# Mixture-of-experts FFN: tokens sorted by expert through a table in DRAM, in place of running every token through every expert

## Chip, core and metric

One core of a Trainium2 chip. The time is the device time in microseconds of one execution of the whole kernel; of several runs of the same kernel the median counts. The profile is taken on one execution; TensorE is PE, VectorE is DVE, ScalarE is ACT, GpSimd is POOL, SyncE is SP (it issues the DMA transfers). PEld is TensorE's weight load.

## The reference

One transformer block on 4 batches of 512 tokens of 256 numbers, all float32. Cut to what matters:

```
h = layernorm(x) * (1 + ca) + sa           # scale and shift per batch, from c
x = x + ga * attention(h)                  # 16 heads of 128, causal
h = layernorm(x) * (1 + cb) + sb
x = x + gb * ffn(h)

ffn(x):
  h = x @ down_w + down_b                  # 256 -> 128
  probs = softmax(x @ router_w + router_b - 1e-7 * cost)
  topv, topi = top_k(probs, 2);  gate = softmax(topv)
  for k in 0, 1:
    for e in 0..7:                         # hidden 128,256,384,512,128,256,384,512
      hm = h * (topi[k] == e)              # a token that e doesn't serve enters as zeros
      acc += gelu(gelu(hm) @ w1[e] + b1[e]) @ w2[e] + b2[e]
    out += acc * gate[k]
  out += 0.1 * (gelu(gelu(h) @ shared_w1 + shared_b1) @ shared_w2 + shared_b2)
  return out @ up_w + up_b + gelu(x) @ core_w + core_b
```

The masked-out tokens of an expert are not absent: each enters as a row of zeros and comes out as gelu(b1) @ w2 + b2, a constant of the expert, its *idle* output. So a token gets from an expert it isn't routed to that constant, times the gates of the two experts it is routed to, and from its own two experts the real output times a gate. An expert serves about a quarter of the tokens; the most that one expert has of one batch's 512, by the inputs that the reference draws, is 237.

## The kernel before, in words

**Numbers.** Products that need full precision are made as three passes of the fast float32r form: each operand is split into a rounded part and a rest, and `mm3` (L149 to L153) multiplies low by high, high by low and high by high into the same PSUM tile. A plain float32 matmul gives the same in one instruction that PE executes as several slower steps.

**Attention.** The loop runs over 64 heads in the order groups of 4 heads x 4 batches (n = 0 to 63), so the last four, n = 60 to 63, are batch 3's. Per head: projections; scores and exp in `weights` (L550: DVE maximum and mask L567, ACT exp L577, DVE reciprocal L581, POOL normalising L582); the transposed weights in `turned` (L585: DVE transposes L597, then DMAs that move blocks of 32 into place and back, `moved` and `aT`); their split in `parted` (L610: ACT L614, POOL through `rest`, L159); the product with the values in `mixed` (L619), and `project_out` (L647), which adds to the residual (DVE L669, POOL L671). LAG = 3 heads lie between a head's scores and its product with the values. After the last head of a batch the second layer norm, its modulation (into h2T, the FFN's input with features in partitions, DVE L418 and transposes L448) and the routing of that batch follow.

**FFN.** `all_ffn` (L1038) goes through the batches in turn; each has 20 chunks of 128 hidden units (1 to 4 per expert, experts in the order 3, 2, 0, 6, 4, 5, 1, 7) and the shared expert as the 21st. A chunk is two products over all 512 tokens: `first` (L880) multiplies the batch's gelu(h), split in two (L848 and L159), with w1 in three passes of 512 columns and takes gelu on ACT (L900, L903); `second` (L925), FFN_LAG = 3 chunks later, multiplies that with w2 into the expert's PSUM tile. In batch 0 and in the 8 chunks of WHOLE the second product is one plain fp32 matmul (L940); in the other 36 chunks `parts` (L906) splits the activations (ACT, DVE `al`) and mm3 follows. When an expert is complete, DVE takes off its idle output and multiplies by the gate of every token (L964, zero where it isn't routed) and POOL adds it to the batch's sum `oacc` (L968). The gates come as a row per expert, spread to all partitions by a DMA (L888) from gates_e in DRAM, which `route` (L678) writes. `route` has the experts in 32 partitions and works in pieces between chunks. `idle_output` (L797) computes the constants with 20 one-column products (L802). `core` (L996) and `outputs` (L1013) follow for the batch before, at chunks 4 to 6: gelu(x) @ core_w, the sum @ up_w, times the gate row, plus the residual (POOL L1027), out to DRAM.

**Order of the work.** The order of PE's instructions is written by hand for the whole kernel. From the FFN on, that of DVE, ACT and POOL is written by hand too (`manual_schedule`, L1312 to L1320); before that a scheduler of the framework decides theirs. Each engine works in order, and all DMAs are issued by SP. FFN weights are split early in the attention (PART_AT, `part_wf`), kept in DRAM and loaded back from head n = 60 on and, by LATE_UNITS, during the FFN.

Of the kernel before, what the change touches and what calls it, by code (L numbers as in the profile page):

```python
# [11 lines left out]
F32 = mybir.dt.float32  # L12
F32R = mybir.dt.float32r
AF = mybir.ActivationFunctionType
# [9 lines left out]
HG = 4  # L24
# [15 lines left out]

WHOLE = (1, 3, 6, 8, 11, 13, 16, 18)
PARTED = tuple(i for i in range(NCH) if i not in WHOLE)

# [3 lines left out]
def runs(blocks):  # L47

    out = []
    for x in blocks:  # L50
# [12 lines left out]
    **{  # L63
        f"second{u}": ([N2 + PLACE[i] for i in PARTED[4 * u : 4 * u + 4]], True)
        for u in range(len(PARTED) // 4)
    },
    "whole": ([N2 + PLACE[i] for i in WHOLE], False),
    "shared": ([2 * NCH, 2 * NCH + 1], True),
    "up": ([2 * NCH + 2, 2 * NCH + 3], False),
    "core": (list(range(2 * NCH + 4, 2 * NCH + 8)), True),  # L70
    "down": ([2 * NCH + 8, 2 * NCH + 9], True),
# [19 lines left out]

LAST_USE = {f"second{u}": PARTED[4 * u + 3] for u in range(len(PARTED) // 4)}
LAG = 3
FFN_LAG = 3
FFN_OUT = 6
GELU_PARTS = (17, 19)
FFN_CORE = (4, 5)
BEFORE3 = 4
EARLY = 2
# [13 lines left out]
PART_AT = (17, 19, 21, 23, 25, 27, 35, 37, 39, 41, 43)  # L113

LATE_UNITS = (
    ("first3", "wu", 0),
    ("second2", "aTh", 2),
    ("first4", "wu", 4),
    ("core", "wu", 4),
    ("shared", "T", 5),  # L120
    ("up", "vf", 6),
)

@with_exitstack
def adaln_attention_moe_kernel(
# [107 lines left out]
    gb1 = const.tile([P, NCH], F32, tag="gb1", name="gb1")  # L233
# [3 lines left out]
    wf_t: dict[str, bass.AP] = {}  # L237
# [11 lines left out]
    def part_wf(u: str):  # L249

        n = len(UNITS[u][0]) * P
        st = staged[u]
        d = parts_d[u] = dram.tile([P, 3, n], F32, tag=f"wfp_{u}", name=f"wfp_{u}")
        if u.startswith("second"):
            nc.sync.dma_start(d[:, 2, :], st)
        hi = work.tile([P, 512], F32R, tag="stage", name=f"hi_wf_{u}")[:, :n]
        nc.scalar.copy(hi, st)
        nc.sync.dma_start(d[:, 0, :], f32(hi))
        rest(nc.gpsimd, st.bitcast(F32R), st, hi)
        nc.sync.dma_start(d[:, 1, :], st)  # L260

    def load_wf(u: str, tag: str = "wu"):
        blocks, in_parts = UNITS[u]
        n = len(blocks) * P
        pool, bufs = (const, 10) if tag == "wu" else (work, 3 if tag == "vf" else 2)
        if not in_parts:
            wf_u[u] = pool.tile([P, n], F32, tag=tag, name=f"wf_{u}", bufs=bufs)
            load_runs(wf_u[u], wf_runs(u))
            return
        t = wf_t[u] = pool.tile([P, 2, 512], F32, tag=tag, name=f"wf_{u}", bufs=bufs)  # L270
        wf_u[u] = t[:, 0, :n].bitcast(F32R), t[:, 1, :n].bitcast(F32R)
        if u.startswith("second"):
            nc.sync.dma_start(t[:, 1, :n], parts_d[u][:, 2, :])
        else:
            load_parts(u)

    def load_parts(u: str):
        n = len(UNITS[u][0]) * P
        nc.sync.dma_start(wf_t[u][:, :, :n], parts_d[u][:, :2, :])
# [28 lines left out]
    router_w = const.tile([P, DC, 2 * E], F32, tag="router", name="router")  # L308
# [13 lines left out]
    with tc.manual_schedule(engines=fixed):  # L322
        nc.vector.memset(mask[:, : NT - 1, :], 0.0)
        nc.vector.memset(router_w, 0.0)
    nc.sync.dma_start(router_w[:, :, :E], router.rearrange("p (c n) -> p c n", n=E))
# [110 lines left out]
    def modulated(b: int, which: int):  # L436
# [28 lines left out]
        if which and b:  # L465
            for c in range(DC):
                turn(c)
                yield
                scaled(c)
                yield  # L470
                parts(c)
            yield
            return
# [200 lines left out]
    routed: dict[int, bass.AP] = {}  # L674

    last_exps: dict[str, mybir.Instruction] = {}

    def route(b: int):  # L678


        n = S // R

        def each(a: bass.AP) -> bass.AP:

            return a.unsqueeze(2).to_broadcast([R, n, E])

        def row(a: bass.AP) -> bass.AP:

            return a.unsqueeze(1).to_broadcast([R, n, E])

        def t2(nm):
            return small.tile([P, n], F32, tag=f"r_{nm}", name=f"r_{nm}_{b}", bufs=1)[:R]

        pl = psum.tile([P, S], F32, tag="pj", name=f"pl_{b}", bufs=3)[:R]
        parts = [(c, a) for c in range(DC) for a in h2T[b]]
        for i, (c, a) in enumerate(parts):
            nc.tensor.matmul(
                pl, lhsT=rw[:, c], rhs=a[:, c, :], start=i == 0, stop=i == len(parts) - 1
            )
        yield  # L700
        lt = work.tile([P, S], F32, tag="stage", name=f"lt_{b}")[:R]
        nc.vector.transpose(lt, pl)
        lt3 = lt.rearrange("p (j e) -> p j e", e=R)
        yield
        lg = small.tile([P, n * E], F32, tag="r_lg", name=f"r_lg_{b}", bufs=1)[:R]
        lg = lg.rearrange("p (j e) -> p j e", e=E)
        nc.vector.tensor_tensor(lg, lt3[:, :, :E], lt3[:, :, E : 2 * E], ALU.add)

        ex, s, hot1, gt = (
            lt[:, i * n * E : (i + 1) * n * E].rearrange("p (j e) -> p j e", e=E) for i in range(4)  # L710
        )
        nc.vector.tensor_tensor(lg, lg, row(rbias[:R]), ALU.add)
        yield
        m, sm, f, g1, g2 = (t2(nm) for nm in ("m", "sm", "f", "g1", "g2"))
        desc = rt[:R, R_DESC - R_ROUTER : R_DESC - R_ROUTER + E]

        def top(hot):
# [3 lines left out]
            nc.vector.tensor_tensor(lg, lg, each(m), ALU.subtract)  # L721
            yield
            nc.vector.scalar_tensor_tensor(s, lg, 0.0, row(desc), op0=ALU.is_ge, op1=ALU.mult)
            nc.vector.tensor_reduce(f, s, AX.X, ALU.max)
            nc.vector.tensor_tensor(hot, s, each(f), ALU.is_equal)

        def exp(to, a, spare):


            if b == 0:  # L730
                last_exps["route"] = nc.scalar.activation(to, a, AF.Exp).ins
                return
            nc.scalar.activation(to, a, AF.Tanh, scale=0.5)
            yield
# [4 lines left out]
        yield from top(hot1)  # L739
        yield  # L740
        yield from exp(ex, lg, gt)
        yield
        nc.vector.tensor_reduce(sm, ex, AX.X, ALU.add)
        nc.vector.reciprocal(sm, sm)
        nc.vector.scalar_tensor_tensor(lg, hot1, -BIG, lg, op0=ALU.mult, op1=ALU.add)
        yield
        yield from top(gt)
        yield


        yield from exp(g1, m, g2)
        nc.vector.scalar_tensor_tensor(g1, g1, 1.0, sm, op0=ALU.subtract, op1=ALU.mult)
        yield
        nc.scalar.activation(g1, g1, AF.Tanh, scale=-0.5)
        yield
        nc.vector.tensor_scalar(g2, g1, -0.5, 0.5, ALU.mult, ALU.add)
        nc.vector.tensor_scalar(g1, g1, 0.5, 0.5, ALU.mult, ALU.add)
        nc.vector.tensor_tensor(hot1, hot1, each(g1), ALU.mult)
        nc.vector.tensor_tensor(gt, gt, each(g2), ALU.mult)
        yield  # L760


        ge = s.rearrange("p j e -> p (j e)")
        nc.vector.tensor_tensor(
            ge.rearrange("p (e j) -> p j e", e=E), hot1, gt, ALU.add
        )
        turned_gt = ex.rearrange("p j e -> p (j e)")
        nc.vector.transpose(turned_gt, ge)
        gates_e = dram.tile([E, S], F32, tag=f"gates_e{b}", name=f"gates_e_{b}")
        nc.sync.dma_start(  # L770
            gates_e.rearrange("(k a) (j r) -> (a j) k r", a=R // n, r=R),
            turned_gt.rearrange("p (k r) -> p k r", r=R),
        )
        routed[b] = gates_e


    def w1(i: int):
        return part(wf_u[f"first{i // 4}"], (i % 4) * P, P) if i < NCH else part(
            wf_u["shared"], 0, P
        )  # L780

    def w2(i: int, b: int):

        if i == NCH:
            return part(wf_u["shared"], P, P)
        if i in WHOLE:
            return wf_u["whole"][:, ts(WHOLE.index(i), P)]
        k = PARTED.index(i)
        if b == 0:
            return wf_t[f"second{k // 4}"][:, 1, ts(k % 4, P)]  # L790
        return part(wf_u[f"second{k // 4}"], (k % 4) * P, P)


    idle = const.tile([P, E], F32, tag="idle", name="idle")
    cvec = const.tile([P, 1], F32, tag="cvec", name="cvec")

    def idle_output(e: int, mine: list[int]):  # L797

        pc = psum.tile([P, 1], F32, tag="pj", name=f"pc_{e}", bufs=3)
        for n, i in enumerate(mine):  # L800
            at = PLACE[i]
            nc.tensor.matmul(  # L802
                pc, lhsT=w2(i, 0), rhs=gb1[:, at : at + 1], start=n == 0, stop=n == len(mine) - 1
            )
        nc.vector.tensor_copy(idle[:, e : e + 1], pc)

    def constant():

        b2s = small.tile([P, 2], F32, tag="b2s", name="b2s", bufs=1)
        nc.vector.tensor_reduce(b2s[:, :1], ct[:, C_B2 : C_B2 + E], AX.X, ALU.add)  # L810
        nc.vector.scalar_tensor_tensor(
            b2s[:, :1], ct[:, C_B2 + E : C_B2 + E + 1], 0.1, b2s[:, :1], op0=ALU.mult, op1=ALU.add
        )
        nc.vector.tensor_reduce(b2s[:, 1:], idle, AX.X, ALU.add)
        nc.vector.tensor_tensor(cvec, b2s[:, :1], b2s[:, 1:], ALU.add)
# [11 lines left out]
    begun: dict[int, mybir.Instruction] = {}  # L827

    beside: list = []

    def next_piece():
# [592 lines left out]
```

## Time and profile before

| | |
|---|---|
| runs | 799.51, 801.11, 802.89 us; median 801.11 |
| the profiled execution | 802.16 us, its span 800.4 us |
| mean granted clock of TensorE | 0.991 |
| first score of head n = 63 (PE) | 600.9 us after the span's start |
| first product of the experts (`ph`, PE) | 608.5 us |
| HBM | 73.05 MB read, 50.14 MB written |

Times in the profile's lines count from the start of the span; 1.76 us of the execution lie around it. A line of a group reads: line of the code, engine, operation, output <- inputs with their shapes, how often | busy time, mean duration of one | idle time of the engine just before them, and what ended it. Matmuls are pipelined, so their durations overlap. A line of a table by stretches reads: stretch, its length, then for PE, PEld, DVE, ACT and POOL the busy time and in brackets the instructions, then the granted clock, the share in which the DMA engines were busy, and GB/s. In a DMA line the last number is the median time in us from issue to landing.

### The profile page before, as it was taken

To read this page: it belongs to the slowest core of one execution; us is meant where nothing else is said; L and a number is where in the kernel's file an instruction comes from. 1 tells how busy PE (TensorE), PEld (TensorE's weight loads), DVE (VectorE), ACT (ScalarE), POOL (GpSimd) and SP (SyncE) were. 2 spreads that over 40 slices of the span, in tenths; PEclk is the share of its full clock that TensorE was granted. 3 is DMA by queue.
4 is the path that set the end of the run, shared out by engine and by line. 5 is a ranking of instruction groups with operands and counts; after the bars stand their busy time and mean duration, and the time that the engine had idled before them with its cause. 6 is when DMAs were issued, how large, how long until landed. Compare 5 with 4: busy or idle time off the path is not lost. (4 is left out here: it accounts for less than half of the span.)

```text
span 800.4 us, 14197 instructions
## 1 busy us (share of the span) xinstructions
PE 777.7 (97%) x4530; PEld 675.6 (84%) x4530; DVE 595.1 (74%) x1736; ACT 511.3 (64%) x1211; POOL 504.1 (63%) x495
## 2 busy tenths in 40 slices
PE   8999999999999999999999999998999989989897
PEld 7899999999999989999999999997897756767575
DVE  6897877777776767776777777787985587868855
ACT  5677677767667677667667767666566335656562
POOL 4466657786665778565768767563565355563765
PEclk9999999999999999999999999999999999999999
DMA  7466455756666667666557656444576331302122
GB/s 252 132 179 196 121 160 151 211 162 193 195 183 202 176 208 188 175 185 194 162 172 205 190 155 189 139 138 133 158 229 203 118 98 54 98 35 75 59 70 62
DMA packets 73354, 124.12 MB, mean 155 GB/s; under 512 B 9136, under 2 KB 51392, under 8 KB 73280
## 3 DMA queue, kind: packets, MB, share of 16 engines
q1 hardware_dynamic: 72864, 123.20, 52.2%
q8 instruction: 36, 0.59, 0.3%
q14 instruction: 38, 0.31, 0.1%
q10 hardware_dynamic: 416, 0.02, 0.0%
HBM read 73.05 MB, written 50.14 MB: 154 GB/s over the span
## 5 line engine op out<-in xcount | busy, mean ns | idle before, releaser
L582 POOL TENSOR_SCALAR e<-e,inv 128x128 f32<-128x128 f32 (+3 forms) x256 | 135.7, 539 | 190.8 <-DVE inv L581 183.5
L577 ACT ACTIVATE e<-e,nmax 128x128 f32<-128x128 f32 (+3 forms) x256 | 143.9, 564 | 67.0 <-DVE nmax L567 66.1
L159 POOL TENSOR_TENSOR aT<-aT,aTh 128x1152 fp32r<-128x1152 f32 x64 | 171.2, 2675 | 16.7 <-ACT aTh L614 9.2
L567 DVE CUSTOM_DVE_ANT_0 e<-ps,mask 128x128 f32<-128x128 f32 (+3 forms) x256 | 122.9, 486 | 56.8 <-PE ps L153 40.5
L597 DVE STREAM_TRANSPOSE T<-e 128x384 f32<-128x384 f32 (+2 forms) x256 | 100.8, 446 | 35.2 <-POOL e L582 35.1
L632 ACT CAST zh<-pz 128x512 fp32r<-128x512 f32 x64 | 37.6, 588 | 78.6 <-PE pz L628 78.4
L614 ACT CAST aTh<-aT 128x1152 fp32r<-128x1152 f32 x64 | 73.1, 1141 | 3.9 <-DMA aT<-moved 3.9
L151 PE MATMUL ps<-kh,ql 128*128 128x256 f32 (+2 forms) x192 | 70.9, 369 | 3.0 <-DVE nmax L567 3.0
L151 PE MATMUL po<-wo,zl 128*128 128x256 f32 x256 | 72.8, 284 | 0.4 <-DVE zl L159 0.4
L152 PE MATMUL pv<-wv,hTh 128*128 128x256 f32 x256 | 72.3, 283 | 0.0
L151 PE MATMUL pv<-wv,hTl 128*128 128x256 f32 x256 | 72.3, 283 | 0.0
L153 PE MATMUL po<-wo,zh 128*128 128x256 f32 x256 | 72.3, 282 | 0.0
L153 PE MATMUL pv<-wv,hTh 128*128 128x256 f32 x256 | 71.9, 281 | 0.0
L152 PE MATMUL po<-wo,zh 128*128 128x256 f32 x256 | 71.7, 280 | 0.0
L153 PE MATMUL pz<-aTh,vh 128*128 128x512 f32 (+2 forms) x192 | 65.3, 340 | 0.0
L152 PE MATMUL ps<-kl,qh 128*128 128x256 f32 (+2 forms) x192 | 65.0, 339 | 0.1
L152 PE MATMUL pz<-aT,vh 128*128 128x512 f32 (+2 forms) x192 | 65.0, 339 | 0.0
L151 PE MATMUL pz<-aTh,vl 128*128 128x512 f32 (+2 forms) x192 | 65.0, 339 | 0.0
L153 PE MATMUL ps<-kh,qh 128*128 128x256 f32 (+2 forms) x192 | 64.8, 338 | 0.0
L968 POOL TENSOR_TENSOR oacc<-oacc,part 128x512 f32<-128x512 f32 x28 | 39.8, 1422 | 38.2 <-DVE part L964 33.6
L581 DVE RECIPROCAL inv<-tot 128x1 f32<-128x1 f32 x256 | 39.8, 157 | 30.4 <-ACT e L577 25.0
L159 DVE TENSOR_TENSOR zl<-pz,zh 128x512 fp32r<-128x512 f32 x64 | 43.8, 684 | 16.4 <-ACT zh L632 16.4
(240 smaller groups left out, 2335.1 us busy)
## 6 DMA issues: line engine op xcount, KB each, us to landing
moved<-T SPq DMA_DIRECT2D x256, 160.0 KB, 2.8
aT<-moved SPq DMA_DIRECT2D x64, 640.0 KB, 3.9
spread<-gates_e SPq DMA_DIRECT2D x32, 256.0 KB, 3.2
st_wqk<-in_wqk SPq DMA_DIRECT2D x16, 256.0 KB, 4.2
wf_first<-wfp_first SPq DMA_DIRECT2D x5, 512.0 KB, 4.5
st_wv<-in_wv SPq DMA_DIRECT2D x8, 256.0 KB, 4.2
st_wo<-in_wo SPq DMA_DIRECT2D x8, 256.0 KB, 3.5
wmod<-in_wmod SPq DMA_DIRECT2D x6, 256.0 KB, 4.4
```

The source lines that it names most:

```text
L151: nc.tensor.matmul(o, lhsT=wl, rhs=mh, start=start, stop=False)
L152: nc.tensor.matmul(o, lhsT=wh, rhs=ml, start=False, stop=False)
L153: nc.tensor.matmul(o, lhsT=wh, rhs=mh, start=False, stop=stop)
L159: return eng.tensor_tensor(lo, full, f32(hi), ALU.subtract)
L567: least = nc.vector.tensor_tensor_reduce(out=et, in0=ps[:, :n], in1=maskf[:, S - n :], scale=-SCALE, scalar=BIG, op0=ALU.add, op1=ALU.min, ...
L577: exp = nc.scalar.activation(et, et, AF.Exp, bias=nm[:, t : t + 1], scale=-1.0, accum_out=tot[:, t : t + 1])
L581: nc.vector.reciprocal(inv[:, one], tot[:, one])
L582: by_sum = nc.gpsimd.tensor_scalar(et, et, inv[:, one], 1.0, ALU.mult, ALU.mult)
L597: nc.vector.transpose(to[:, first : first + n], blocks[:, at : at + (n - 1) * step + 1 : step])
L614: nc.scalar.copy(hi, full)
L632: recent["z"] = nc.scalar.copy(zh.rearrange(by_block, a=NB, r=R), pz).ins
L968: recent["added"] = nc.gpsimd.tensor_tensor(oacc, oacc, to, ALU.add).ins
```

## The change

Each batch's tokens are placed by expert in a table of 8 x 256 rows of 128 numbers in DRAM, and an expert works only on its 256 rows. The steps, per batch:

- `clear` (twelve DMAs in all, from head n = 36 on, one per head) fills the tables with zeros. Place 0 of each expert stays empty: it yields the idle output.
- `down_and_route`: h = x @ down_w + b stays unsplit (dF), and `route` now has tokens in partitions: 16 products of 16 columns, one step after the other without pieces. It gives gates, and for each token the two experts (hot2).
- `by_token` transposes h so that a token is a row (dtok); `bring` computes each token's place by products with a triangle and with ones (the count of tokens before it with the same expert), and sends the rows to the table with eight indirect DMAs, issued by POOL, 128 rows of 512 bytes each. It also notes whether an expert has more than 255 tokens.
- `Sparse`: per pair of experts `get` reads 512 rows back with four DMAs (runs of 128 bytes), `turn` transposes them on DVE, takes gelu (ACT), and splits (DVE). A chunk is three passes of 256 columns; the second product is two plain fp32 matmuls of 128 x 128 with the activations as weights, so its output has tokens in partitions. A pair's output goes by one DVE copy and one DMA to a second table, `given`.
- `take`: eight indirect DMAs, issued by POOL, fetch each token's two rows; ACT and DVE scale and add them. `add_idle` adds, in one PSUM tile, the idle outputs times (1 - gate) (one plain fp32 product) and the transposed rows, to the shared expert's output.
- The dense path over all 512 tokens stays as `all_experts`, in a branch at the very end that runs only if an expert had more than 255 tokens of a batch; a flag is reduced, loaded into a register on each engine and compared.

Around it: the second weights aren't split any more (unsplit loads, seven splits in PART_AT for eleven), `idle_output`, the spread gates, L964 and L968 are gone; `manual_schedule` for DVE, ACT and POOL in the FFN is gone, so that a scheduler orders them there too; PE's order is still written. The norm, routing and `bring` of batches 0 and 1 lie among the last heads of the attention, those of 2 and 3 among the chunks of batches 0 and 1. `take(0)` comes at chunk 26 of 80, `take(1)` at 46, `take(2)` at 66, `take(3)` behind the last.

```diff
+PLACES = 256
+    def bring(b: int):
...
+        nc.tensor.matmul(pp, lhsT=tri, rhs=mn, start=True, stop=False)
+        for t in range(NT - 1):
...
+        places[b] = small.tile([P, 2 * NT], I32, tag="places", name=f"places_{b}", bufs=B)
+        nc.vector.tensor_copy(places[b], at_sum.rearrange("p k t -> p (k t)"))
+        for t in range(NT):
+            for k in range(2):
+                sent = nc.gpsimd.indirect_dma_start(
+                    table[b][:, :],
+                    bass.IndirectOffsetOnAxis(ap=places[b][:, k * NT + t : k * NT + t + 1], axis=0),
+                    dtok[b][:, t, :],
+                    None,
+                ).ins
...
+    class Sparse:
+        def get(self, i: int):
+            for a in range(NB):
+                nc.sync.dma_start(
+                    got[a * R : (a + 1) * R].rearrange("r (j l) -> r j l", l=R),
+                    table[self.b][i * S : (i + 1) * S, a * R : (a + 1) * R].rearrange(
+                        "(j r) l -> r j l", r=R
+                    ),
+                )
+        def turn(self, i: int):
+            nc.vector.transpose(full, self.got[i])
+            nc.scalar.activation(full, full, AF.Gelu)
+            nc.vector.tensor_copy(hi, full)
+            rest(nc.vector, lo, full, hi)
+        def second(self, k: int, hid, acc):
+            for t in range(tiles):
+                nc.tensor.matmul(
+                    acc[:, half * self.n + t * L :][:, :L],
+                    lhsT=hid[:, ts(t, P)],
+                    rhs=w2(k),
...
+            nc.vector.tensor_copy(y, acc)
+            nc.sync.dma_start(given[self.b][i * S : (i + 1) * S, :]...
+    def take(b: int):
+        for t in range(NT):
+            for k in range(2):
+                nc.gpsimd.indirect_dma_start(
+                    y[:, k, t, :],
+                    None,
+                    given[b][:, :],
+                    bass.IndirectOffsetOnAxis(ap=places[b][:, k * NT + t : k * NT + t + 1], axis=0),
+                )
+            nc.scalar.activation(y[:, 0, t, :], y[:, 0, t, :], AF.Copy, scale=g[:, 0, t : t + 1])
+            nc.vector.scalar_tensor_tensor(y[:, 0, t, :], y[:, 1, t, :], g[:, 1, t : t + 1], ...
+    def add_idle(b: int, also: str = ""):
+        nc.tensor.matmul(po, lhsT=idle[0], rhs=lefts[b], start=True, stop=got is None)
+        for t in range(NT if got is not None else 0):
+            nc.tensor.matmul(
+                po[:, ts(t, P)], lhsT=got[:, 0, t, :], rhs=ident, start=False, stop=t == NT - 1
+            )
+        nc.vector.tensor_tensor(sums[b], sums[b], po, ALU.add)
...
         if b < 2:
             later.setdefault(n + 3, []).append((modulate, b, 1))
-        if b == 0:
-            later.setdefault(n + 4, []).append((all_of, route, b))
+            later.setdefault(n + 4, []).append((down_and_route, b))
+            later.setdefault(n + 5, []).append((by_token, b))
+            later.setdefault(n + 6, []).append((bring, b))
...
-    ctx.enter_context(tc.manual_schedule(engines={DVE, Activation, Pool}))
...
+    nc.vector.tensor_reduce(flags[:, :1], over, AX.X, ALU.max)
+    nc.vector.tensor_copy(flag, flags[:, :1])
+    missing = nc.values_load(flag[:1, :1], min_val=0, max_val=1)
+    with tc.If(missing > 0):
+        all_experts()
```

## Prediction

> **What bounds the kernel now.** I read the page's busy table first, then the granted clock, the busy time by stretches of the FFN, the forms of the FFN's matmuls, the chain that ended last with the timeline behind it, and the waits.
>
> ```profile
> span 800.4 us, 14197 instructions
> PE 777.7 (97%) x4530; PEld 675.6 (84%) x4530; DVE 595.1 (74%) x1736; ACT 511.3 (64%) x1211; POOL 504.1 (63%) x495
> ```
>
> PE is busy 97% of the span; nothing else is over three quarters. The stretches of the FFN (length, then busy time of PE, PEld, DVE, ACT, POOL, then clock and DMA):
>
> ```profile
> 600.00:610.00 10.00, 8.95 (x53) 7.57 (x52) 7.28 (x24) 6.80 (x14) 7.87 (x8) 1.00 0.81 278
> 610.00:630.00 20.00, 19.63 (x113) 15.64 (x110) 5.62 (x10) 10.37 (x15) 6.52 (x3) 1.00 0.38 107
> ...
> 667.00:707.00 40.00, 37.09 (x160) 26.94 (x158) 36.49 (x72) 24.21 (x40) 23.99 (x19) 1.00 0.25 80
> 707.00:747.00 40.00, 38.51 (x160) 28.06 (x160) 29.70 (x49) 21.04 (x36) 20.25 (x16) 0.96 0.16 53
> 747.00:793.00 46.00, 43.09 (x193) 31.98 (x191) 29.78 (x38) 27.61 (x44) 32.61 (x25) 1.00 0.20 64
> 793.00:800.40 7.40, 1.99 (x8) 1.44 (x8) 3.31 (x8) 0.00 (x0) 1.40 (x2) 1.00 0.21 71
> ```
>
> PE leads in each but the last. Only between 667 and 707 does DVE come near it (36.5 of 40). DVE, ACT and POOL have some 5 to 20 us of slack per batch, because PE is slow: that cover is what the change takes away.
>
> ```profile
> L151 PE MATMUL ph<-ghh,wf_first 128*128 128x512 f32 x80 | 42.1, 526 | 1.6 <-DVE ghh L848 0.8 <-ACT hid L900 0.8
> L940 PE MATMUL acc<-hid,wf_whole 128*128 128x512 f32 x64 | 33.6, 607 | 0.5 <-DVE part L964 0.5
> ```
>
> Durations in these rows overlap; what counts is the step from one issue to the next. The timeline gives .233 us for a pass of 512 columns (603.21, 603.44, 603.67), .118 for 256 (790.39, 790.51, 790.63), .86 for a plain fp32 matmul of 512 columns (two records) and .21 for one of 128.
>
> **PE's sum.** The stage starts with the first score of the last head (n=63), at 600.9, and ends at 800.4: 199.5 us. A chunk costs PE 3 x .233 = .70 for its first product and .86 (44 chunks) or .70 (36) for its second; after the change 3 x .118 + 2 x .21 = .78 for both. Eighty chunks: 119.1 before, 62.4 after. Twenty columns for idle tokens (L802, about 3 us) go. New in the stage are add_idle (4 x 1.7), turn_gates (4 x .44), by_token (3 x .44), router products of 16 columns instead of 512 (about level) and prefix matmuls (3 x .6). down, shared, core, up and the last heads stay; down and routing of batch 0 move ahead of head 63 and make 3.4 us there. Adding each matmul in its written order at these steps gives 172.8 us before and 123.0 after. The stage had 199.5 - 172.8 = 26.7 us without an issue: 8.3 behind the last expert, 18.4 spread. Kept as it is, that would make 800.4 + 3.4 - 49.8 = 754. So the question is how much waiting is added.
>
> **What takes PE's place.** In the new stage, from the first sparse chunk on, I add each queue by nearest rows. DVE: per batch four transposes of 128x512 (.69, L702 has 32x512 in .693), four hi copies, four lo differences and four y copies (.69 each, L848), in all 11 us, with the sums, gates and outputs and two late norms and routings: 96 us. ACT: 20 gelus of 256 columns (half of L900's .684 and its fixed part, .42), 4 of 512, core, shared: 73. POOL: 37 us of additions (L994, L975, L1027: 1.3 to 1.5 each) and 56 indirect transfers. PE: 112. Four queues within a factor of 1.5, each waiting on the others in order, replace one that led by far.
>
> **The price of an indirect transfer, g.** No indirect and no POOL-issued DMA is in the trace. The nearest rows:
>
> ```profile
> L413 POOL TENSOR_TENSOR rstd<-rstd,minus_half 128x4 f32<-128x4 f32 x7 | 7.5, 1065 | 0.4
> L159 POOL TENSOR_TENSOR aT<-aT,aTh 128x1152 fp32r<-128x1152 f32 x64 | 171.2, 2675 | 16.7 <-ACT aTh L614 9.2
> ...
> moved<-T SPq DMA_DIRECT2D x256, 160.0 KB, 2.8
> ...
> gates_e<-lt SPq DMA_DIRECT2D x4, 16.0 KB, 1.4
> ```
>
> Below, an issue on SP takes .32 us; above, POOL's longest instruction takes 2.7. I take g = 1.1, next to a slow small POOL operation (1.065), and 2 us of landing between the 1.4 and 2.8 of the last two rows. With it POOL has 37 + 62 = 99 us. A hold-up by DVE would come on top: with both inputs in SBUF, DVE's al takes 992 ns instead of the 692 of ghl from PSUM, so sharing with POOL already shows.
> [...]
>
> **The sum.** I followed the written order of PE and the in-order queues of the others, each at its row.
> 1. Start of head 63: +8.5 (600.9 to 609.4). 3.4 us is PE's moved work; the rest is 9 us more of DVE (second norm, modulation and routing of batch 1 now in heads 60 to 63; between 580 and 600 DVE was 16.45 of 20 us busy) and eight scatters of bring(0), 8.8 us, in front of the normalisations (L582) in POOL's queue. Those 183.5 us that POOL waited at L582 give room for part. Without room it is +13, with all hidden +3.4.
> 2. Turn to the experts: before, chunks fill the last heads' waits from 608.5. After, the first chunk needs the table read back (1.4 to 2.8 landing), transposed, through gelu and split, behind head 63's 18 us of DVE work. PE has 11 us for it: 7.5 idle, first sparse chunk at 628.
> 3. The middle: 98 us of PE's work to the last expert matmul. The scatters of batch 1 (8.8 and 2 landing) hold DVE, which waits in order at the first transpose of batch 1, so the shared expert of batch 0 comes about 10 late. By batch 2's first chunk 77.5 us pass for 54.5 of work; from there 9 more for the gathers of take and the tables of batches 2 and 3. Together 32 idle, 18.4 before.
> 4. Tail: last expert matmul at 758; copy of y .7, its write 2, eight gathers 8.8, landing 2, scale and combine 1, add_idle, core and up of batch 3 to the output's landing 8.5 = 23, with 14 of PE's work in it: 9 idle, 8.3 before.
>
> ```profile
> 788.78 0.86 PE acc L940 x2
> 790.41 0.76 DVE part L964
> 791.32 1.29 POOL oacc L968
> 793.16 2.01 PE py L1022 x8
> 795.65 0.87 DVE y L1035
> ```
>
> This is the present tail, from the chain of waits; the gathers stand in place of the one POOL addition.
> So 800.4 + 8.5 - 49.8 + (7.5 + 32 + 9 - 26.7) = 780.9. The profiled run took 802.16, 1.76 more than its span, 1.05 over the median of 801.11. With the 1.76 I get 782.7, on the median's scale **782 us**, 2.4% faster. About 28 of the 56 indirect transfers lie on this path (4 of bring(0), 8 each of bring(1), one take in the middle, take(3)), so each .1 us of g is worth 2.8 us: 760 at .32, 827 at 2.7, 801 (no change) at 1.8.
>
> **Free edits, and their covers.** The clearing writes, 4.7 MB more on SP's queue from n=36 on, lie beside DMA at 52% mean; 12 issues of .32 to .43 are hidden unless the moved and aT transfers (landing 2.8, 3.9) come later, at worst +1 a piece, 12. Reading the tables, 64 transfers of 128-byte runs: gates_e with such runs landed in 1.4, but 64 KB has four times its runs, so 1.4 to 2.8 and at worst 4 us more at each of four first tables. Fewer weight splits and .32 issues: below 1 us gained. Flag and branch at the end: one DVE reduction and copy (.15 to .3 each) and a load of a register: .5 to 2, beside the last outputs' landing. The order that a scheduler gives DVE, ACT and POOL instead of the written one: -5 to +15, in the range, 0 in the sum.
> A clock drop is the other cost of idling: behind PE's wait at 703 to 707 passes ran at .43 instead of .233 (710.34, 710.77, 711.20) and the stretch shows .96. Three such waits cost some 1.5 to 2 us each, but where PE waits anyway they are hidden; 0 to +5.
>
> **Rivals.**
> A. The indirect transfers cost about .5 us and the waits stay as before: PE bounds, and 754 + 1.8 = 756, to 765. For it: POOL's total slack. Against: step 2 needs no g to be idle.
> B. Slower. One mechanism: an indirect transfer holds POOL for 2 us or more, each scatter and gather in front of its additions; POOL then has 37 + 112 = 149 us in the stage and leads it. It decides from g = 1.8 on; at 2.0 to 2.7 it gives 807 to 827, 812 likeliest. For it: POOL's rows are the longest in the trace. Against: those rows move 1152 elements per partition, an indirect transfer's list 128 numbers.
> C. The cross waits of DVE's new order decide with g near 1.4: 790 to 799, a gain below 2%.
> D. Not what it says: an expert with over 255 tokens in a batch calls the dense path, at least 80 x 1.56 = 125 us behind all: over 900. The reference's inputs, routed, give at most 237, so 1%.
>
> **Chances.** Forecast (766 to 789) .45, A .20, C .15, B .14, no change (797 to 805, between C and B) .05, D .01. Half a per cent, 4 us, is about what a measurement tells from no change. Faster .45 + .20 + .12 (C below 797) = .77; same .03 + .05 = .08; slower .15. The range of 8 in 10 takes in A's 753 and C, and B to 810.
>
> **What would show it.** Right: first sparse ph 19 us behind head 63's first score; PE near 90% busy but with holes of 5 to 10 us at batch 1's first transposes and at the end; POOL's indirect transfers about 1.1 us apart; last expert matmul near 758. A: PE without holes, gathers .5 apart. B: POOL with no gaps from bring(1) on and everything late behind it. Wrong altogether if head 63 begins later than 615, where the attention, not the FFN, was hurt.

## The result, and the profile after

The changed kernel takes **846.9 us** (four runs, 842.5 to 847.7) where the kernel before took 800.3 beside it: a ratio of **1.057 (1.052 to 1.061)**. Forecast were 782, with a range to 810; it went to the other side. The profiled execution took 846.27 us, its span 844.6.

The head of the page, to be held against the one of before:

```profile
span 844.6 us, 14869 instructions
PE 760.2 (90%) x4771; PEld 689.9 (82%) x4771; DVE 581.0 (69%) x1812; ACT 492.7 (58%) x1221; POOL 502.5 (59%) x522
```

TensorE's busy time fell by 17.5 us only and the span grew by 44. The groups of instructions show that the chunks became as small as was planned (80 chunks, passes of 256 columns, two products of 128 x 128 per chunk, each of which makes two records: the 256 of L991 below and 64 more with `wf_second_up`):

```profile
L991 PE MATMUL acc_s<-wf_second,hid_s 128*128 128x128 f32 x256 | 44.8, 304 | 1.7 <-DVE y_s L1001 1.7
L144 PE MATMUL ph_s<-gxh_s,wf_first 128*128 128x256 f32 x80 | 31.2, 390 | 35.4 <-DVE act_shared L1062 22.0 <-DVE gxh_s L966 5.4 <-DVE zl L152 4.0
...
L832 POOL DMA_INDIRECT table<-dtok,places x32 | 31.4, 980 | 22.2 <-DVE places L828 13.6 <-issue 8.5
L1088 POOL DMA_INDIRECT taken<-given,places x32 | 30.8, 962 | 18.3 <-DMA given<-y_s 9.1 <-issue 8.8 <-PE ph_s L146 0.3
```

The first product of a chunk now stands behind 35 us of waiting; before it was 1.6. An indirect transfer holds GpSimd .96 to .98 us, and .30 more pass before the next: 1.26 from one to the next, in runs of eight (10 us) or sixteen (20 us).

The busy time by stretches, cut at the marks of the prediction (head 63's first score, first sparse chunk, last expert product; columns as shown of before):

```profile
612.70:639.30 26.60, 14.06 (x86) 12.89 (x85) 21.57 (x77) 13.19 (x27) 15.21 (x13) 0.81 0.72 194
639.30:814.20 174.90, 126.58 (x834) 117.38 (x835) 85.89 (x197) 71.93 (x156) 81.25 (x77) 0.82 0.32 75
814.20:844.60 30.40, 19.03 (x93) 15.11 (x90) 10.64 (x20) 2.05 (x5) 11.47 (x12) 0.77 0.21 63
```

In the middle no engine is near full: TensorE 127 of 175 us, and part of that at half clock (granted .82 over the middle; .50 from 635.95 to 649.6, where passes of 256 columns stand .21 us apart, against .12 behind that). Here is the account by stage that all that follows uses, read at the same marks in each trace, in us:

| kernel | head 63 starts | turn | middle | tail | span |
|---|---|---|---|---|---|
| before | 600.9 | 7.7 | 183.9 | 7.9 | 800.4 |
| forecast | 609.4 | 18.6 | 130 | 23 | 781 |
| after | 612.7 | 26.5 | 175.0 | 30.3 | 844.6 |
| after_third (same kernel, another chip) | 611.4 | 25.3 | 152.3 | 31.5 | 820.5 |

The turn is the time from the first mark to the second, the middle from the second to the third, the tail what follows. In after the middle gave 9 us where 54 were forecast, and the start, the turn and the tail cost 12, 19 and 22. TensorE's waits from the turn on, from the view of waits of after (in total, times, longest):

```profile
PE ph_s L144 <- DVE act_shared L1062: 22.0, 4, 13.4
PE ph_shared L144 <- ACT hid_s L922: 11.0, 2, 10.8
PE po L144 <- DVE r_g L705: 7.2, 1, 7.2
PE ph_s L144 <- DVE gxh_s L966: 5.4, 1, 5.4
```

Two of these waits are over 10 us long (13.4 and 10.8). The tail, from the chain that ended last:

```profile
814.88 0.34 DVE taken L1096
...
827.02 0.35 DVE taken L1096
827.37 2.05 issue
829.49 1.09 DVE taken L1096
...
835.43 1.71 PE py L1170 x8
837.25 0.76 DVE y L1183 x2
838.00 0.58 DVE y L1185
```

Where before there were two operations and an output, a batch is combined, turned and projected twice (batches 2 and 3), the second time behind its gathers.

### The profile page after: what moved, and what is told of

Its sections match the earlier page's. It is cut to its first block, busy times and chain, and to the rows that moved or that the text cites. A ratio compares the mean times of both kernels' runs of the same rounds, so it can differ in the third digit from the quotient of the medians.

```text
span 844.6 us, 14869 instructions
## 1 busy us (share of the span) xinstructions
PE 760.2 (90%) x4771; PEld 689.9 (82%) x4771; DVE 581.0 (69%) x1812; ACT 492.7 (58%) x1221; POOL 502.5 (59%) x522
## 4 chain that ended last, share of the span: by engine, by line
PE 76%; DVE 8%; DMA 4%; issue 3%; ACT 3%; another core or an unknown queue 3%; POOL 1%; SPq 1%; DVEq 0%; ACTq 0%; POOLq 0%
PE ps L144 4%; PE ps L145 4%; PE ps L146 4%; PE pz L144 3%; PE pz L145 3%; PE pz L146 3%; PE acc_s L991 3%; PE pk L145 3%; PE pk L146 3%; PE pk L144 3%; PE pv L144 3%; PE pv L145 3%; PE pv L146 3%; PE po L144 3%; PE po L146 3%; PE po L145 3%
## 5 line engine op out<-in xcount | busy, mean ns | idle before, releaser
L152 POOL TENSOR_TENSOR aT<-aT,aTh 128x1152 fp32r<-128x1152 f32 x64 | 171.4, 2678 | 14.7 <-ACT aTh L586 7.3
L922 ACT ACTIVATE hid_s<-ph_s,cols 128x256 f32<-128x256 f32 x80 | 37.1, 474 | 59.0 <-PE ph_s L146 32.5
L144 PE MATMUL ph_s<-gxh_s,wf_first 128*128 128x256 f32 x80 | 31.2, 390 | 35.4 <-DVE act_shared L1062 22.0
L553 DVE RECIPROCAL inv<-tot 128x1 f32<-128x1 f32 x256 | 40.1, 159 | 30.2 <-ACT e L549 24.9
```

Of the source, the lines that this page charges most:

```text
L144: nc.tensor.matmul(o, lhsT=wl, rhs=mh, start=start, stop=False)
L152: return eng.tensor_tensor(lo, full, f32(hi), ALU.subtract)
L553: nc.vector.reciprocal(inv[:, one], tot[:, one])
L922: nc.scalar.activation(hid, ph, AF.Gelu, bias=b1[:, PLACE[k] : PLACE[k] + 1])
```

## Experiments

Theory at first: the indirect transfers cost more than their own time; in stretches with them the end of an instruction reaches its waiter late (a *late signal* from here on: an engine stands idle although what it waits for ended microseconds ago). Rivals: it is GpSimd's time that counts; it is the waits that the new structure has anyway; it is the half clock behind the waits. A fifth suspect was the clearing. From the timeline of SyncE's queue in after:

```profile
5.63 2.98 SPq L766 DMA_DIRECT2D table<-mask  x4
14.61 6.54 SPq L766 DMA_DIRECT2D table<-mask  x8
```

The clearing writes are not at head 36 and later, where they are written, but at the very start: nothing on SyncE's queue held them back. The heads lag before by 2.1 us at head 4 and 6.3 at head 8, and keep it.

**Clearing held back.** In e3 the clearing waits behind a late aT transfer:

```
-        nc.sync.dma_start(aT, ...)
+        recent["aT"] = nc.sync.dma_start(aT, ...).ins
...
+        with tc.issue_after(recent["aT"]):
             nc.sync.dma_start(rows_t..., mask...)
```

> The changed kernel with the twelve zero-filling transfers queued on SyncE behind those of heads 36 on, where the code has them, and not at the kernel's start, where the trace has them (5.6 to 21 us). If their place delays the first loads and with them the first eight heads, the lag of head 8 (6.3 us) goes to about 1 and the whole to 841 us (5 to 6 less than 846.9). Rival: the lag of the first heads has another cause, or the fill costs as much among the later heads: within 2 us of 846.9.

Measured: 820.1, ratio 1.023 (1.019 to 1.028), 27 us less than after. That was too much for 6 us of lag, and no late signal was left in the trace.

**Plain transfers.** In e1 SyncE moves the same bytes in fixed rows (the placing by expert is left out), in e2 GpSimd, in e7 SyncE with e3's clearing:

```
-    nc.gpsimd.indirect_dma_start(table[b][:, :], bass.IndirectOffsetOnAxis(ap=places...), dtok[b][:, t, :], None)
+    nc.sync.dma_start(rows_j[2 * t + k], dtok[b][:, t, :])    # e2: nc.gpsimd; the gathers likewise
```

> The changed kernel with its 64 indirect transfers replaced by plain ones of the same size and row length (128 rows of 512 bytes, spread over the whole table), issued by SyncE. It leaves out the placing by expert: tokens go to fixed rows. Theory 1 (while GpSimd issues indirect transfers, the end signals of TensorE's matmuls reach the other engines late, by up to 9 us, and the clock halves in the waits): 780 to 800 us, no wait of ScalarE on a matmul that ended 5 us before. Theory 2 (the order of the queues and the waits between them cost it, whoever issues the transfers): 825 us or more, holes in TensorE like those of the changed kernel. In between if both hold.

> The 64 transfers plain as in the run issued by SyncE (810 us; no placing by expert), but issued by GpSimd. If an indirect transfer costs as GpSimd's own transfer: within 8 us of the changed kernel of this call. If it's the list of rows that costs: within 8 us of 810.

> Plain transfers on SyncE and the late fill together (no placing by expert). If both count by themselves: 810 - 6 = 804 us, 16 below the late fill with indirect transfers; that difference is then what GpSimd's issuing costs. Rival: the late fill's gain of 27 us was mostly the end of late signals, which plain transfers have not either: 804 all the same, so only the heads' lag tells; if it is above 809, the fill costs among the later heads.

Measured: e1 809.8, ratio 1.010 (1.007 to 1.013); e2 815.2, 1.016 (1.012 to 1.020); e7 804.3, 1.003 (1.001 to 1.005). No late signals in any. Issued by GpSimd instead of SyncE the same plain transfers cost 5 us, by runs on two chips; e2's trace also has an operation of VectorE held for 10.5 us (more on such holds below), e1's middle none of over 2.5. Against e3, e7 is 16 us less: the price of indirect transfers on GpSimd, the index and the issuing engine together. And e7, free of all that, is no faster than before: the work that TensorE was spared is eaten by something else.

**Bursts in the kernel before.** e4 adds eight indirect gathers (unused) in GpSimd's queue in batches 1 to 3, e5 as much plain GpSimd work in the same place:

```
+                if b and k == 9:
+                    burst(b)    # e4: 8 x indirect_dma_start; e5: a memset and 7 multiplications
```

> The kernel before with eight indirect loads of 128 rows of 512 bytes, whose data nobody uses, issued by GpSimd in one go at chunk 9 of batches 1, 2 and 3. Theory 1: signals of TensorE come late in the 10 us of each burst, with holes of 3 to 8 us in TensorE: 812 to 825 us, and at least 6 us above the same kernel with plain GpSimd work in the same place. Theory 2: the burst costs only GpSimd's time, 10 us three times, nearly all hidden: 800 to 806, as with plain work.

> The control of the former: in place of each burst one memset and seven multiplications of 128x512 on GpSimd (about 10 us). Both theories: 800 to 806 us; above 806, the hold of GpSimd's additions itself costs TensorE time, and the burst has to be read against this number.

Measured: 821.4, ratio 1.023 (1.020 to 1.027), and 816.6, 1.019 (1.015 to 1.022). Without late signals, 9 to 10 us of GpSimd's time cost some 5 to 6 us of the path each, in the old kernel, of whatever kind. So the hold on GpSimd alone is a price. The indirect kind adds 5 us in three bursts, each of which is also longer (about 10 us against 9).

**Same kernels, another chip.** After once more, on chip 5, and e6, which is e3 with the shared expert's gelu in SBUF so that the next third chunk gets its PSUM tile sooner:

```
-        nc.scalar.activation(ph, ph, AF.Gelu, bias=b1[:, NCH:])
+        act = work.tile([P, S], F32, tag="tmp", name=f"gelu_shared_{b}")
+        nc.scalar.activation(act, ph, AF.Gelu, bias=b1[:, NCH:])
```

> The changed kernel once more, unaltered, beside the others of this call. In its trace ScalarE's gelus start up to 9 us after the matmul that they wait for, while GpSimd issues indirect transfers; in the variant with the late fill, whose FFN has the same instructions in nearly the same order, none do, and its FFN is 24 us shorter. If the early fill makes that: 847 us again, with such late starts. If it belonged to that execution or that chip: 825 to 830 us (the late fill's 820 and the first heads' 6).

> The changed kernel with the late fill, and the shared expert's gelu written to SBUF and not in place in PSUM, so that the next chunk's matmul has the PSUM tile when ScalarE's gelu ends and needn't wait for VectorE's split. In the late fill's trace TensorE waits 13.6 us in four places for that split. If these waits are a cause: 806 to 812 us. Rival: the late signals and gathers decide and the next wait takes their place: 817 to 823.

Measured: 845.2, ratio 1.053 (1.049 to 1.057), and 838.6, 1.044 (1.040 to 1.048), both with late signals. I read this at first as a property of the program, since e3 and e4 had none; but those two had run on chip 11. The next four went to chip 11 together:

> The changed kernel as it is, a third time, on the same chip and beside e3_again. The late signals (an end on TensorE, VectorE or ScalarE that its waiter sees 2 to 11 us later, in stretches with indirect transfers) were in every trace of the changed kernel and of e6_shared_sbuf, and in none of e3_clear_late and e4_before_burst; but the first two ran on other chips than the last two. If the lateness belongs to the program: 843 to 848 here with late signals, and e3_again without them. If it belongs to the chip that a program falls on: both with or both without; without them 822 to 828 here (that is 820 and the 6 us of the early clearing).

> The kernel of e3_clear_late (clearing behind the heads, the rest as the change has it) once more, on the chip of after_third. Lateness by program: 816 to 823, no late signal. Lateness by chip: as late as after_third, 836 to 842 with late signals if after_third has 845, and 816 to 823 without them if after_third has 825.

Measured: after_third **823.5**, ratio 1.028 (1.025 to 1.031); e3_again 817.3, 1.020 (1.018 to 1.021). Neither has a late signal. The unchanged kernel is 22 us faster on this chip; the kernel before is level on all (800 to 802). So it is the chip, or the occasion, together with indirect transfers: late on chips 5 and 2 and in the first run (its chip is not on record), in every kernel with indirect transfers; not late on chip 11; and never with plain transfers (chips 11, 5 and 9). The clearing at the start costs 6 us, the difference of the two.

What a late signal looks like, first in after (all engines' timeline, the tokens' transposes of batch 2). A row gives start and duration; in brackets stands the engine's idle time before it and what ended that, "remote" where the profile shows no sender:

```profile
703.57 0.92 PE L802 MATMUL ptk<-ident,dF 128*128 128x128 f32 x4
...
704.61 0.96 POOL L1088 DMA_INDIRECT taken<-given,places  x1 [0.30 <-issue]
...
712.25 0.47 ACT L922 ACTIVATE hid_s<-ph_s,cols 128x256 f32<-128x256 f32 x1 [7.15 <-remote]
...
715.80 0.69 DVE L804 COPY dtok<-ptk 128x512 f32<-128x512 f32 x1 [10.22 <-remote]
```

then the same instructions, in the same order, in after_third:

```profile
698.15 0.66 PE L802 MATMUL ptk<-ident,dF 128*128 128x128 f32 x4
...
698.84 0.69 DVE L804 COPY dtok<-ptk 128x512 f32<-128x512 f32 x1 [1.73 <-PE ptk L802]
```

The copy follows the transposes within .03 us there; in after it starts 11.3 us behind their end, and VectorE is idle for the last 10.2 of these, while GpSimd's gathers run on at 1.26 us each. From the records I can say that the semaphore is seen late (7 to 12 us at worst, by trace); what delays it they do not show. The traces with late signals also lack records: e2's trace has 1,024 landing signals for its 64 plain transfers, 16 for each; for the 64 indirect ones after's trace holds 248 (248 to 276 in every trace with late signals), after_third's 1,021. Every timed run was recorded, so whether the recording itself has a part in the delay was not tested.

**The half clock.** In e3_again 51 us of TensorE's work run at half clock from 578 us on. e8 fills eight of the waits with unused products:

```
+        for _ in range(n):
+            nc.tensor.matmul(pw, lhsT=ident, rhs=ident, start=True, stop=True)    # n = 28, 20, 20, 20, 9, 9, 20 and 6 + 16
```

> e3_clear_late, with plain 128x128 multiplications of the identity (their results unused) in front of eight of TensorE's waits: 28 before the first product of head 62's second part behind the last head (a wait of 6.3 us), 20 before the first sparse chunk (4.7), 20, 20, 9 and 9 before the four chunks that wait for the shared expert's split (4.7, 4.6, 2.2, 2.2), 20 before batch 1's core product (4.7), 6 and 16 in the tail. At .21 us each they fill the waits and are no longer than these. If the half clock behind the waits costs time: in e3_clear_late 46 us of TensorE work run at half clock; some 28 of them lie behind these eight waits, so 10 to 14 us less, a ratio to e3_again of .983 to .988. If the other engines set the pace there and TensorE only waits elsewhere for what it gains: within 3 us of e3_again, or later by some of the 30 us of added products.

Measured: 824.9, ratio 1.029 (1.027 to 1.031), 8 us **later**. The middle, first in e3_again, then in e8:

```profile
633.60:784.90 151.30, 126.38 (x834) 117.08 (x835) 92.95 (x197) 72.08 (x154) 81.26 (x77) 0.86 0.37 87
```

```profile
640.30:792.00 151.70, 134.66 (x990) 125.15 (x991) 90.39 (x198) 70.19 (x153) 79.52 (x76) 0.94 0.37 86
```

The clock went from .86 to .94, and the middle took the same 151 us; TensorE only waited elsewhere for what it gained: less the 78 products added there (.21 us each, 16 us) its busy time fell from 126 to 118 us. Of the 8 us that the whole lost, 5 are the turn, where the added 28 products were longer than their wait (30.9 us instead of 26). In after the granted clock is .50 behind TensorE's waits of 4.9 to 13.4 us (the 5.38 us before 639.28 among them), but also behind one of 2.09 us (before 826.70), and not behind one of 2.17 (before 749.55). This case shows, as far as e8 filled the waits, that the fall need not cost anything.

**Gathers or scatters; the shared split; the table's way.** e9 is e3 with plain gathers and indirect scatters, e13 is e7 with e6's edit, e14 is e7 without its scatters:

> e3_clear_late, with the 32 gathers of take as plain transfers of 64 KB on SyncE's queue (rows in a fixed order, so the outputs are not combined by token), and the 32 scatters still indirect on GpSimd's. From e3_clear_late (820) to e7_sp_late (804), where both are plain, 16 us went. If the gathers hold the path, three at 8 to 10 us in line behind the scatters or at the end: 806 to 809. If the scatters do, in front of the tables that the first products of each batch need: 814 to 818. On a chip or in a program with late signals both are later by their share of some 20 us, which then goes with the kind of transfer that is left.

> e7_sp_late (clearing late, all transfers plain and on SyncE's queue, no placing by expert, so no late signals on any chip so far) with the shared expert's gelu in SBUF, so that the next third chunk gets its PSUM tile one operation after the product. In e7_sp_late TensorE waited 11.6 us in four places for that split. If these waits are on the path: ratio .990 to .996 (793 to 797). If the other engines set the pace and the wait moves elsewhere: 1.000 to 1.006.

> e7_sp_late with the 32 scatters left out: the tables keep their zeros, so the experts work on zeros, but with the same reads, transposes, gelus, splits, products and gathers. What goes is the chain by which a batch's first tables wait for the routing: scatter, its landing, reading. If that chain sets the turn and the heads of the batches: the turn 19 to 21 us instead of 25, the middle 8 to 15 us shorter than 143, ratio .975 to .985 (782 to 790). If the engines' in-order work (two norms and routings, splits, the batches' ends) sets them, with or without tables: ratio .996 to 1.004.

Measured: e9 814.6, ratio 1.015 (1.014 to 1.017), 3 us less than e3_again, so that of the 13.5 us between e3_again and e7 (1.020 to 1.003) some 10 go with the scatters, or with what else changes with them: in e9 one operation of VectorE is held for 6.8 us, in e7's middle none. e13 800.1, ratio .998 (.996 to 1.000): 4 us less than e7, between the two expectations. e14 799.4, .998 (.995 to 1.001): 4 to 5 us less than e7, with the turn as long as ever (25.8) and the middle 7 shorter; head 63 began 3.9 us later, for a reason not looked into. With the scatters goes, by the edit, the order that kept the work beside the chunks behind them. The account by stage:

| kernel | head 63 starts | turn | middle | tail | span |
|---|---|---|---|---|---|
| e3_again | 607.6 | 26.0 | 151.2 | 30.2 | 815.1 |
| e9_gather_direct | 607.5 | 24.8 | 151.6 | 28.3 | 812.3 |
| e7_sp_late | 605.1 | 25.0 | 143.1 | 26.1 | 799.2 |
| e13_sp_shared | 605.3 | 24.8 | 138.7 | 27.8 | 796.6 |
| e14_no_scatter | 609.0 | 25.8 | 136.2 | 25.8 | 796.8 |

**Three repairs.** They fell on chip 2, with late signals, and so can be compared with each other only. e10 moves batch 1's routing and scatter into the FFN, e11 takes the core's bias off GpSimd, e12 is both with e6's edit:

```
-        if b < 2:
+        if b < 1:    # e10; batch 1: {0: next(m1) twice, 1: down_and_route, 2: by_token, 4: bring} beside the chunks
...
-            nc.gpsimd.tensor_tensor(xu, xu, pair(gbias), ALU.add)
+            nc.tensor.matmul(py[:, t, :], lhsT=ones[:1], rhs=obias[0][:1], start=False, stop=False)    # e11
```

> The kernel of e6_shared_sbuf once more (clearing behind the heads, the shared expert's gelu into SBUF). There it ran among late signals, 838 with the changed kernel at 845. On a chip without them e3_clear_late has 817 to 820 with 10.5 to 13.6 us of TensorE's waits for the shared split in it. If these waits are on the path: 808 to 812. If the other engines' queues set the pace, as e8_warm suggests, and the wait only moves: 815 to 822. With late signals again 836 to 843.

> e3_clear_late with batch 1's modulation, routing, turn and scatter in the first five chunks of the FFN instead of in heads 62 and 63 and behind them. If VectorE's routing of batch 1, ahead of the last head's work in its order, is what makes the turn 25 us instead of the 18.6 of the prediction: the wait of 6 us at the product of head 62's second part goes, the first sparse chunk comes 18 to 20 us behind head 63's first score, and the whole takes 808 to 814, if the scatter of batch 1 stays early enough for its first chunk. If the turn is set by batch 0's own chain (its table's way back, transpose, gelu, split): 24 us and within 3 us of 817 to 820; if batch 1's tables then come late, 820 to 828.

> e3_clear_late with the core's bias added to the accumulator by a plain product of a row of ones with the bias row on TensorE (16 of 256 columns, .43 us each, 7 us), instead of multiplied by the gate and added to x by GpSimd (12 operations, 13 us of GpSimd). In the trace of after_third VectorE's split of batch 1's core input (128x512) took 7.08 us from 759.22, while GpSimd ran six of these additions back to back (758.40 to 765.74); TensorE waited 7.8 us for it. If additions of GpSimd on SBUF keep VectorE's operations on SBUF out, and this sits on the path: that split takes 1.3 or less, the wait goes, 809 to 813. If not: the split stays long, or the time within 3 us of 817 to 820.

> e3_clear_late with the edits of e6_shared_sbuf, e10_one_later and e11_bias_by_pe together. If each of the three waits is on the path, 5 to 8 us each: 797 to 803, level with the kernel before (802). If the middle is set by GpSimd's runs of scatters and gathers (16 in line, 20 us, twice) and by the order of VectorE: 808 to 816.

Measured: 840.9 (ratio 1.049, 1.047 to 1.051), 848.8 (1.058, 1.055 to 1.061), 852.9 (1.063, 1.058 to 1.067) and 858.8 (1.074, 1.070 to 1.079). None helps. In e10 the turn is 22.0 instead of 25.7; the wait for r_g (6.4 us in e6_again) has become one of 6.0 us for another operation of VectorE, zl. But the middle is 13 us longer than in e6_again (which also has e6's edit). Batch 1's first chunk does not wait for its tables; it is the first five chunks, with batch 1's routing now beside them, that take 24.4 us instead of 14.7. In e11 no operation of VectorE is held for the core's bias any more (below), but the tail took 39 us, with 17 us of TensorE's work in it at half clock. What these edits give on a chip without late signals was not tried.

The hold that e11 was made for, in after_third, GpSimd's and then VectorE's timeline:

```profile
758.40 7.34 POOL L1142 TENSOR_TENSOR x<-x,gbias 128x512 f32<-128x512 f32 x6
```

```profile
759.22 7.08 DVE L152 TENSOR_TENSOR gxl<-gx,gxh 128x512 fp32r<-128x512 f32 x1
```

A subtraction that takes .69 us elsewhere takes 7.08, until GpSimd's run of six additions is over. On chip 2 the order differs and another operation is held, in e6_again (VectorE's, then GpSimd's timeline):

```profile
762.17 8.05 DVE L1098 SCALAR_TENSOR_TENSOR taken<-taken,g 128x128 f32<-128x128 f32 x1 [0.23 <-ACT taken L1097]
```

```profile
762.70 7.37 POOL L1144 TENSOR_TENSOR x<-x,gbias 128x512 f32<-128x512 f32 x6
```

In e10 the same one takes 7.50. In e11 and e12, on the same chip and without these additions, no operation of VectorE takes more than 2.7 us from head 63 on. And in e7, beside the run of six from 707.39 to 714.82, VectorE's operations with an input in PSUM go through in their usual time:

```profile
713.30 0.69 DVE L1108 TENSOR_TENSOR sum<-sum,po_idle 128x512 f32<-128x512 f32 x1 [2.30 <-PE po_idle L1105]
```

So VectorE was held for a whole run of six (7.08 and 8.05 us), not for the rest of one addition (1.25 us).

## Why the prediction was wrong

Point by point, by its own steps; after_third is the kernel without late signals.

- **g, the price of an indirect transfer: right.** 1.26 us from one to the next against 1.1; at the 28 transfers put on the path this is 4.5 us. Below the 1.8 at which rival B decides, so the slowdown is not B. VectorE did not hold the transfers up: their issues took .94 to 1.31 us, beside whatever VectorE did (after_third).
- **PE's work: right in kind, short in size.** Middle: 123.4 us busy, 33 of them at half clock, make 107 at full clock (123.4 - 33/2), forecast 98.
- **Step 3, "together 32 idle": this step failed.** The middle took 152.3 us in after_third, 22 over the forecast of 130. 9 are the work above, 13 more are lost time: 45 us instead of 32. Of the 45 TensorE is idle for 29, and 16 are what the half clock adds; they are counted together because e8 made less of the one, got as much more of the other and gained nothing. Taken away step by step, scatters by index were worth 8 us of the middle (e9 to e7), the way through the table 7 (e7 to e14), the shared expert's split in PSUM 4 (e7 to e13). The prediction had the first two and no term for the third, nor for VectorE held by GpSimd's additions (an operation of 7.1 us in after_third). What this last is worth is not shown: in e7 it is gone too, and may be part of the 8, and e11 ran among late signals only.
- **And it had no term for late signals**: on the chips of the result another 22.7 us, all in the middle (175.0 against 152.3; the other stages differ by 1.3 at most). No row of before could show them, since it has no indirect transfer. It is half of what the middle missed, and a third of the whole miss (844.6 against 781).
- **Step 2, the turn: mis-sized, 25 to 26.5 us instead of 18.6.** The prediction let VectorE's 18 us of work for head 63, with the first table's way back behind it, set it. The way back does not: e14 has no scatter to wait for and the same turn. VectorE's queue has a part in it: it is busy 21 of the turn's 25.3 us in after_third, and with batch 1's routing moved out (e10) 12.9 of 22.0. One of its operations, of .19 us where nothing holds it, is held there too, beside GpSimd's split of the attention's weights (after_third):

```profile
629.40 2.65 DVE L699 TENSOR_TENSOR hot<-r_s,r_f 128x32 f32<-128x32 f32 x1
```

```profile
629.34 2.67 POOL L152 TENSOR_TENSOR aT<-aT,aTh 128x1152 fp32r<-128x1152 f32 x1
```

What sets the 22 us that are left in e10 stays open.

- **Step 4, the tail: mis-sized, 30.3 instead of 23.** 19 us of TensorE's work instead of 14, since two batches, not one, are finished behind the last expert. With plain transfers 26 to 28.
- **Step 1, head 63: nearly right**, 612.7 and 611.4 against 609.4, but in part by luck: 4 us of it (611.4 against 607.6 in e3_again) are **the clearing, put at nothing in the sum, under "free edits"**. Its cover was looked for at head 36, and it ran at the start. Without it the start would have been below the forecast.
- **The clock, "0 to +5, hidden where PE waits anyway": right as far as e8 goes.** It cut TensorE's work at half clock in the middle from 39 to 16 us, and the middle stayed as long; the 16 that were left were not tried.
- **The rivals.** C, the cross waits of the new order, is nearest in kind, but its range ends at 799; without late signals the kernel takes 823.5.
- **"Wrong altogether if head 63 begins later than 615": not the case.** The FFN, not the attention, was hurt.

In sum, for after_third: 2 us (start) + 6.7 (turn) + 22.3 (middle) + 8.5 (tail) = 39.5 over the forecast span of 781; for after 24 more. What sets the remaining middle of e14 (136 us for some 107 of work), with no transfer by index and no scatter, was not taken apart further: the four engines wait for each other in turn. What delays the signals stays open as well.

## What to carry to other kernels

When one engine is busy 97% and a change takes a quarter of a stage from it, price the ends of the stage: the work there is a chain from engine to engine, and here a 41 us shorter middle (e7, without the placing) was given back at the start (4), the turn (17) and the tail (18). Check where a transfer with no wait really runs, not where it is written, and run a kernel with a new kind of transfer on more than one chip before explaining its trace. Filling waits to keep a clock up paid nothing here, where other engines set the pace.

## What was not expected of the hardware

- Semaphores seen up to 7 to 12 us late beside indirect transfers, on some chips and not on another, with the same program (847 and 823.5 us).
- VectorE held for 7 to 8 us by a run of six GpSimd additions of 1.25 us each (7.08 us in after_third, 8.05 in e6_again); beside such a run in e7 its operations with an input in PSUM passed (.69 us).
- An indirect transfer of 128 rows of 512 bytes costs GpSimd 1.26 us, and lands some 2.5 us behind its issue (after_third; 2.2 to 4.9).
